# Seven block products instead of row products in the second attention layer of six images

## The chip, the cores and the metric

The kernel runs on one core of a Trainium2 chip. Its time is the device time of one execution in microseconds (us). Three runs of the kernel before gave 2307.95, 2308.07 and 2308.5 us; the median, 2308.07 us, is the time that the change is measured against. TensorE is written PE, VectorE DVE, ScalarE ACT, GpSimd POOL and SyncE SP, as in the profile.

## What is computed

Eight images of 32 x 32 positions (N = 1024 rows) and C = 256 channels pass two attention layers, all in fp32. Layer 0 has four heads of width 256; Layer 1 has one head with keys and queries of width 32 (Ck) and a gate gamma:

```
# layer 0: q, k, v = split(x W_qkv) per head
a   = softmax(q k^T * C**-0.5);  x1 = concat_h(a v) W_out + b_out + x
# layer 1
f, g, h = x1 Wf + bf, x1 Wg + bg, x1 Wh + bh
s   = softmax(g f^T);  out = gamma * (s h) + x1
```

## The kernel before

The work goes image by image. Layer 0 treats each head in two blocks of 512 queries (blk 0 and 1). Its three large products, scores, products with the rows of x, and output projection, are each done as seven block products instead of eight (Strassen-Winograd), by `seven` (L235). Its three tasks `one`, `two`, `three` multiply into three banks of PSUM named z, y and x (in the profile psz, psy, psx with the tile's name behind: psz_y for the products, psz_o for the output projection); ACT copies the first results out (L278, L279, L286), and DVE adds bank and copy into the output tile (L272). The sums of blocks that such a product needs as operands are made on DVE: `query_sums` (qs, L555), `sums` of the exponentials (tile ss, L614), sums of y (tile yt, L692), each 256 or 1024 values wide per partition.

The sum of exponentials over the keys of a block takes a long way in Layer 0: DVE adds over the key tiles (rs, L621, L625), POOL adds over the partitions (`partition_all_reduce` into rb, L627), a DMA on SP writes one row of that into DRAM (line, L631), a second one reads it back as four columns (st, L634), DVE inverts them (`invert`, L643), a DMA writes the inverses back to DRAM (inv, L648), and one more spreads that row over the 128 partitions (invb, L650). Then DVE multiplies the projected tile by it (L701), and POOL's DMA adds it onto x1 in transposed form (x1T, L704). SP issues in order; a DMA that waits for another holds all behind it. Of the buffers rs, rb, invb, ss and m0 there is one each, of s, v, q, y and st two.

Layer 1 of image b-1 is put between heads 1 and 2 of image b (behind all four heads in the last image, and at the very end for image 7). x1T is turned into rows of x1 (`turn_back`: SP's DMAs at L382 and transposes on DVE at L394). `queries_apart` (L751) multiplies x1 by Wf and Wg together; the result is spread by DMAs. `values` (L796) multiplies x1 by Wh, and DVE writes gamma times the result plus gamma times bh into v, with a column of ones beside it (L804). `scores` (L810) has two tasks per block. Each is four matmuls that use 32 rows of the array each, into four of the six PSUM banks "ps"; ACT takes the exponential of each bank into s (L830). `row_products` (L902) then takes, per group of 128 queries, eight matmuls of 257 columns (256 of v and the ones, L909), so that the sum of exponentials comes out in column 257; DVE inverts it (L917) and adds the scaled product to the rows of x1 (the line behind it); the store to the output follows from `done`.

The order on PE, DVE and ACT is written out by hand. A loop goes through the steps (unit, block); in each one `put(tasks, *positions)` places tasks at positions of a scale from 0 to about 10, and the tasks are issued sorted by position. Each step issues its own scores, the products of the step before (`one`), and the projection of the step before that (`two`). For image b the steps are h0 and h1 (both blocks each), Layer 1 of image b-1 (both blocks), h2, h3. SP and POOL get their DMAs in the order in which the tasks issue them.

At the end `judge` and `decide` count whether all inverses lie inside given bounds (FAR for Layer 1); if not, a general path is run.

Of the kernel before, what the change touches and what calls it, by code (L numbers as in the profile page):

```python
# [20 lines left out]
def kernel(  # L21
# [67 lines left out]
    FAR = 2.0**64  # L89
# [265 lines left out]
    xT_of, x1T_of, xblocks, vblocks = {}, {}, {}, {}  # L355
# [81 lines left out]
    def value_sums(b):  # L437

        made = {}

        def piece(i):
            if i == 0:
                r = rows[b]
                t = tile_of("xt", [P, 4, NT // 2, P], f"xt_{b}")
                blocks = [r[:, ts(j, NT // 2), ts(c, P)] for j in range(2) for c in range(CC)]
                sums = [t[:, k] for k in range(4)]
                made["l"] = sum_b(sums, *blocks)
                vblocks[b] = b_operands(blocks, sums)
            made["l"][i]()

        return [partial(piece, i) for i in range(4)]
# [58 lines left out]


    class Layer0:
# [82 lines left out]
        def sums(self, blk):  # L595


            n = f"{self.name}_{blk}"
            tt = nc.vector.tensor_tensor
            made = {}  # L600

            def start():
                half = NT // 2
                p = self.p[blk]
                blocks = [p[:, ts(j, half), ts(e, HB)] for e in range(2) for j in range(2)]
                t = tile_of("ss", [P, 2, half, HB], f"ss_{n}")
                sums = [t[:, 1], t[:, 0], blocks[2], t[:, 0]]
                self.pblocks[blk] = a_operands(blocks, sums)
                made["t"], made["l"] = t, sum_a(sums, *blocks)

            def piece(i):
                if i == 0:
                    start()
                made["l"][i]()  # L614

            def add(k):
                t = made["t"]
                if k == 1:
                    made["r"] = tile_of("rs", [P, 2, HB], f"rs_{n}")
                r = made["r"]  # L620
                tt(r, t[:, :, 0, :] if k == 1 else r, t[:, :, k, :], ALU.add)  # L621

            def last():
                r = made["r"]
                tt(r[:, 0, :], r[:, 0, :], r[:, 1, :], ALU.add)  # L625
                self.total[blk] = t = tile_of("rb", [P, NB], f"rb_{n}")
                nc.gpsimd.partition_all_reduce(  # L627
                    t, r.rearrange("p e i -> p (e i)"), P, bass_isa.ReduceOp.add
                )
                line = tile_of("line", [1, NB], f"line_{n}")  # L630
                nc.sync.dma_start(line, t[0:1, :])  # L631
                self.r[blk] = st = tile_of("st", [P, HT], f"st_{n}")
                with nc.allow_non_contiguous_dma(reason="a row of sums turns into columns"):
                    nc.sync.dma_start(st, line.rearrange("o (t p) -> p (o t)", p=P))  # L634

            adds = [partial(add, k) for k in range(1, NT // 2)]
            return [partial(piece, i) for i in range(4)], adds + [last]

        def invert(self, blk):

            n = self.first + blk * HT
            inv = inverse[:, n : n + HT]
            nc.vector.reciprocal(inv, self.r[blk])  # L643
            if blk in self.rb:
                return
            line = tile_of("line", [1, NB], f"inv_{self.name}_{blk}")
            with nc.allow_non_contiguous_dma(reason="columns turn into a row"):
                nc.sync.dma_start(line.rearrange("o (t p) -> p (o t)", p=P), inv)  # L648
            self.rb[blk] = t = tile_of("invb", [P, NB], f"invb_{self.name}_{blk}")
            nc.sync.dma_start(t, line[0].partition_broadcast(P))  # L650
# [6 lines left out]
        def products(self, blk):  # L657


            def out(c, e):  # L660
                if blk not in self.y:
                    self.y[blk] = tile_of("y", [P, CC, NB], f"y_{self.name}_{blk}")
                return self.y[blk][:, c, ts(e, HB)].unsqueeze(1)

            return seven(
                f"y_{self.name}_{blk}", HB, 1,
                lambda number: [
                    (0, vblocks[self.b][number][:, j, :], self.pblocks[blk][number][:, j, :])
                    for j in range(NT // 2)
                ],  # L670
                {
                    "11": partial(out, 0, 0), "12": partial(out, 1, 0),
                    "21": partial(out, 0, 1), "22": partial(out, 1, 1),
                },
                NARROW,
            )
# [42 lines left out]
    class Layer1:  # L719
        scale = 1.0  # L720

        def __init__(self, b, direct=0):

            self.b, self.name, self.direct = b, f"{b}_l1", direct
            self.s = {}
            self.fg, self.v = None, None

# [23 lines left out]
        def queries_apart(self, tag=None):  # L751
# [7 lines left out]
            def task():  # L759
                fg = self.fg_tile()  # L760
                self.f, self.g = fg[:, 0, :], fg[:, 1, :]
                if tag is None:
                    self.v = values_tile(f"v_{self.name}")
                    made["t"] = t = self.v.rearrange("p t c -> p (t c)")[:, :NB]
                else:
                    made["t"] = t = tile_of(tag, [P, NB], f"fg2_{b}")
# [29 lines left out]
        def values(self, last="psm"):  # L796
            def start():
                if self.v is None:
# [5 lines left out]
                lambda t2, pm: nc.vector.scalar_tensor_tensor(  # L804
                    self.v[:, 2 * t2 : 2 * t2 + 2, :C], pm, gamma_sb,
                    bh_sb.unsqueeze(1).broadcast_to([P, 2, C]), ALU.mult, ALU.add,
# [40 lines left out]
        def products(self, blk):  # L847
            return row_products(self, blk, rows1)

# [116 lines left out]
    steps, adds, exps = [], {}, {}  # L966

    for b in range(B):
        units = [Layer0(b, h) for h in range(HEADS)]
        if b > 0:  # L970
            units.insert(behind(b), Layer1(b - 1, NBLK))
        steps += [(u, blk) for u in units for blk in range(NBLK)]
# [9 lines left out]
    first_sums = value_sums(0)  # L982
# [10 lines left out]
    for i, (a, blk) in enumerate(steps):  # L993
# [7 lines left out]

        if l0:
            tasks, exps[i] = a.scores(blk)
            put(tasks, 0, 2, 4, 6, 8, 10)
            put(exps[i][:2], 5.1, 6.1)
        else:
            tasks, _ = a.scores(blk)
            put(tasks, *((0.5, 2.4) if blk == 0 else (0.5, 2)))
        if is_l0(two):
            u, k = two  # L1010
            put(u.products_of[k][2:], 1 if l0 else 0)
            if nxt is None:
                put([partial(u.invert_all, k)], 2.2)
            put([partial(u.invert, k)], 3.4 if l0 else 2.7)
            ysums, tasks, adds[i] = u.project(k)
            put(ysums, *((1.1, 1.2, 1.3, 3.3) if l0 else (1.1, 1.2, 1.3, 2.5) if blk == 0 else
                         (0.6, 0.7, 0.8, 0.9)))
            put(tasks, *((3, 5.5, 7) if l0 else (4.5, 6, 7.2) if blk == 0 else
                         (3, 5, 7) if nxt else (1.9, 3.1, 4.1)))
            if nxt is None:  # L1020
                put(adds[i], 4.2)
        if i - 1 in exps:
            put(exps[i - 1][2:], *((0.9, 0.91) if l0 else (0.1, 0.2)))
        if i - 1 in adds:
            put(adds[i - 1], 0.5 if l0 or blk == 1 else 2.3)
        if is_l0(one):
# [3 lines left out]
            put(sums, *((2.1, 3.2 if is_l0(two) else 2.4, 4.2, 5.6) if l0 else (0.8, 2.2, 3.5, 6.1)))  # L1030
            put(keys, *((6.3, 6.6, 7.6, 8.7) if l0 else (6.3, 7.6, 8.3, 8.7)))
            put(u.products_of[k][:2], *((5, 9) if l0 else (4, 5)))
        elif one is not None:
            put(one[0].products(one[1]), *((3, 5, 7, 9) if l0 else (1, 4, 6, 8) if nxt else (1, 3, 4, 8.5)))
# [3 lines left out]
        if i == 1:  # L1038
            put(first_sums[2:], 1.4, 3.4)
            put(fold[2], 0.5, 2.6, 3.5, 5.5, 7.5)  # L1040
            put([partial(nc.vector.tensor_scalar, bh_sb, bh_sb, gamma_sb, None, ALU.mult)], 8.5)

        if l0 and blk == 0:
            put(a.query_sums(1), 3.5, 4.3, 4.4, 5.3)
        if is_l0(nxt) and blk == NBLK - 1:
            put(nxt[0].queries(), *((2.5, 4.5, 6.5) if not l0 else
                                    (1.5, 2.5, 4.5) if is_l0(two) else (0.5, 2.5, 5.5)))
            put(nxt[0].query_sums(0), *((6.7, 6.9, 7.3, 7.6) if not l0 else
                                        (5.4, 6.4, 7.2, 7.4) if is_l0(two) else (6.4, 7.2, 7.3, 7.4)))
# [3 lines left out]
        if l0 and a.h == 0 and blk == 1 and a.b > 0:  # L1053
            put(value_sums(a.b), 1.4, 2.4, 3.4, 4.4)
        if l0 and a.h == 1 and blk == 0 and a.b + 1 < B:
            load_x(a.b + 1)
        if is_l0(nxt) and nxt[0].h == 2 and nxt[1] == 0 and nxt[0].b + 1 < B:
            moves, turned = turn_rows(nxt[0].b + 1)
            put(moves[:4], 1, 2.5, 4, 5.5)
        if l0 and a.h == 2 and a.b + 1 < B:  # L1060
            if blk == 0:
                put(moves[4:], 0.5, 1.5, 2.5, 3.5)
                put(turned, 6.4, 7.4, 8.4, 9.4)
            else:
                put(key_sums(a.b + 1), 0.5, 0.6, 6.4, 7.4)

        if l0 and a.b > 0 and a.h == behind(a.b) - 1:
            if blk == 0:
                moves, turned1 = turn_back(a.b - 1)
                put(moves[:4], 3, 4.5, 6, 7.5)  # L1070
            else:
# [3 lines left out]
                put(moves, 1.6, 1.7, 1.8, 1.9)  # L1075
        if not l0 and blk == 0:
            put(a.values("ps"), 0.9, 1, 2.3, 3, 6.5)
            put(turned1, 2.5, 2.9, 4.2, 5.1)
        for _, _, t in sorted(places, key=lambda x: x[:2]):
# [151 lines left out]
```

## Time and profile before

| | |
|---|---|
| median of the runs | 2308.07 us |
| profiled execution: time | 2307.59 us |
| profiled execution: span | 2305.4 us |
| granted TensorE clock | 1.00 |
| PE busy | 2296.3 us, 10256 records |
| DVE busy | 1507.7 us, 2663 |
| ACT busy | 758.9 us, 1297 |
| POOL busy | 319.9 us, 206 |
| all-reduces on POOL | 64 of 3.23 us |

The span is the time from the first to the last instruction; 2.2 us of the execution lie outside it. An fp32 matmul leaves two records, so 10256 records are 5128 matmuls. The matmuls overlap in part: the distance between two starts (the pitch), and not the length of a record, is what a matmul costs. In a timeline a row is a run of the same instruction: start, time from its start to its end, engine, line, operation, output and input with shapes, and the number of records; in brackets stands how long the engine was idle before it, and who ended that.

### The profile page before, as it was taken

The numbers are of one execution on the slowest core, as the hardware profiler recorded it, in microseconds if no ns is written. First come the engines' busy times: TensorE is split into PE (matmuls) and PEld (weight loads), VectorE is DVE, ScalarE is ACT, GpSimd is POOL, SyncE is SP. The second block draws the span as 40 slices with busy tenths as digits, with TensorE's granted clock in tenths as the row PEclk, the third lists the DMA queues.
The fourth block names the chain that finished last, engine by engine and source line by source line (L and its number), as shares of the span: only waits on it lengthen the run. The fifth ranks groups of instructions, "written<-read, shape, count | busy, mean of one in ns | idle before, by whom it ended". The sixth has DMA issues, their size and how long they took to land.

```text
span 2305.4 us, 27193 instructions
## 1 busy us (share of the span) xinstructions
PE 2296.3 (100%) x10256; PEld 1890.9 (82%) x10256; DVE 1507.7 (65%) x2663; ACT 758.9 (33%) x1297; POOL 319.9 (14%) x206
## 2 busy tenths in 40 slices
PE   9999999999999999999999999999999999999999
PEld 7888888788888888878887888878888788888887
DVE  6676776476765766656765566656676556776664
ACT  3333333233332333323333233322333233333322
POOL 0111112011120112101121011210112101111211
PEclk9999999999999999999999999999999999999999
DMA  4211112301223013220132211322013211121222
GB/s 137 33 28 28 27 33 49 75 15 28 42 46 67 15 28 52 42 61 15 28 57 40 59 15 28 58 38 59 19 28 54 46 33 19 28 46 26 38 41 65
DMA packets 240379, 94.81 MB, mean 41 GB/s; under 512 B 204464, under 2 KB 209456, under 8 KB 240240
## 3 DMA queue, kind: packets, MB, share of 16 engines
q1 hardware_dynamic: 220784, 55.23, 12.1%
q0 software_dynamic: 19456, 37.76, 9.3%
q8 instruction: 83, 1.36, 0.4%
q14 instruction: 56, 0.46, 0.1%
HBM read 29.76 MB, written 8.65 MB: 17 GB/s over the span
## 4 chain that ended last, share of the span: by engine, by line
PE 99%; ACT 1%; DVE 0%; issue 0%; ACTq 0%
PE psy_y L255 14%; PE psz_y L255 14%; PE psz L255 14%; PE psy L255 14%; PE pa_l L909 10%; PE psz_o L255 7%; PE psx_y L255 5%; PE psx L255 5%; PE psz_q L255 4%; PE psy_q L255 4%; PE pr_v_l L494 3%; PE ps_l L821 1%; PE psx_q L255 1%; PE psx_o L255 1%; PE pm_fg L771 1%; ACT x1T L459 0%
## 5 line engine op out<-in xcount | busy, mean ns | idle before, releaser
L627 POOL PARTITION_ALL_REDUCE rb<-rs x64 | 206.6, 3228 | 1463.0 <-issue 1078.9
L576 ACT ACTIVATE p<-p 128x1024 f32<-128x1024 f32 x256 | 263.9, 1056 | 71.4 <-DVE p L272 71.2
L255 PE MATMUL psz<-q,xs 128*128 128x256 f32 x1024 | 264.5, 381 | 0.0
L255 PE MATMUL psy<-qs,xs 128*128 128x256 f32 x1024 | 262.8, 379 | 0.0
L255 PE MATMUL psy_y<-p,xt 128*128 128x256 f32 x1024 | 241.9, 379 | 0.0
L909 PE MATMUL pa_l<-v_l,s_l 128*128 128x257 f32 x1024 | 232.1, 381 | 0.0
L255 PEld LDWEIGHTS psz<-q,xs 128*128 128x128 f32 x1024 | 192.8, 190 | 46.8 <-issue 19.1
L909 PEld LDWEIGHTS pa_l<-v_l,s_l 128*128 128x128 f32 x1024 | 193.7, 190 | 34.3 <-issue 6.8
L278 ACT COPY e<-psz 128x512 f32<-128x512 f32 x128 | 75.1, 587 | 437.3 <-PE psz L255 437.3
L255 PEld LDWEIGHTS psy_y<-p,xt 128*128 128x128 f32 x1024 | 194.6, 190 | 26.4
L255 PEld LDWEIGHTS psy<-qs,xs 128*128 128x128 f32 x1024 | 193.6, 190 | 27.4
L272 DVE TENSOR_TENSOR p<-psy,v 128x512 f32<-128x512 f32 x128 | 88.1, 688 | 85.1 <-ACT v L286 44.9
L704 POOL DMA_DIRECT2D x1T<-o x64 | 78.1, 1220 | 405.9 <-DVE o L701 345.2
L255 PE MATMUL psy<-qs,x0T 128*128 128x256 f32 x512 | 131.4, 379 | 0.0
L255 PE MATMUL psx<-q,x0T 128*128 128x256 f32 x512 | 131.4, 379 | 0.0
L255 PE MATMUL psz<-q,x0T 128*128 128x256 f32 x512 | 131.4, 379 | 0.0
L255 PE MATMUL psz_y<-ss,xt 128*128 128x256 f32 x512 | 121.0, 379 | 0.0
L255 PE MATMUL psx_y<-p,x 128*128 128x256 f32 x512 | 121.0, 379 | 0.0
L255 PE MATMUL psz_y<-ss,x 128*128 128x256 f32 x512 | 121.0, 379 | 0.0
L255 PE MATMUL psy_y<-ss,xt 128*128 128x256 f32 x512 | 121.0, 379 | 0.0
L255 PE MATMUL psz_y<-p,x 128*128 128x256 f32 x512 | 121.0, 379 | 0.0
L255 PEld LDWEIGHTS psz_y<-p,x 128*128 128x128 f32 x512 | 97.3, 190 | 20.9 <-issue 4.3
(146 smaller groups left out, 3689.5 us busy)
## 6 DMA issues: line engine op xcount, KB each, us to landing
x1T<-o POOLq DMA_DIRECT2D x64, 512.0 KB, 5.0
invb<-inv SPq DMA_DIRECT2D x63, 256.0 KB, 4.8
x<-x1T SPq DMA_DIRECT2D x256, 32.0 KB, 2.0
out_dram<-x SPq DMA_DIRECT2D x15, 512.0 KB
x<-in_x_dram SPq DMA_DIRECT2D x14, 512.0 KB, 4.4
x0T<-x SPq DMA_DIRECT2D x224, 32.0 KB, 2.3
fg<-v_l POOLq DMA_DIRECT2D x56, 64.0 KB, 2.0
w<-in_L_conv_W_qkv_dram SPq DMA_DIRECT2D x4, 512.0 KB, 7.5
```

The source lines that it names most:

```text
L255: nc.tensor.matmul(banks[k][:, ts(i, w)], lhsT=lhsT, rhs=rhs, start=first and n == 0, stop=True, skip_group_check=True,)
L272: nc.vector.tensor_tensor(dst, shaped(banks[k]), shaped(other), ALU.add)
L278: nc.scalar.copy(scratch("e"), banks["z"])
L494: nc.tensor.matmul(pm[:, ts(j, C)], lhsT=src()[:, c, ts(2 * t2 + j, P)], rhs=w()[:, c, :], start=(c == 0), stop=(c == CC - 1),)
L576: exp(both, both)
L627: nc.gpsimd.partition_all_reduce(t, r.rearrange("p e i -> p (e i)"), P, bass_isa.ReduceOp.add)
L704: nc.gpsimd.dma_start(x1T_of[self.b][:, :, ts(blk, NB)], o, accum_op=ALU.add)
L771: nc.tensor.matmul(pm[ts(k, half)], lhsT=w[:, c, :], rhs=x1T_of[b][:, c, ts(k, NB)], start=(c == 0), stop=(c == CC - 1),)
L821: nc.tensor.matmul(pm, lhsT=self.f[ts(r, CK), ts(j0 + r, P)], rhs=self.g[ts(r, CK), ts(blk, NB)], start=True, stop=True,)
L909: nc.tensor.matmul(pm[:, : C + 1], lhsT=p[:, j, ts(ti, P)], rhs=v[:, j, : C + 1], start=(j == 0), stop=(j == NT - 1),)
```

## The change

Layer 1 of images 0 to 5 no longer makes values first. Since s (x1 Wh) = (s x1) Wh, it multiplies s by the rows of x1, as seven block products, and projects the result by Wh (already scaled by gamma) behind that. Image 6's and image 7's Layer 1 keep the old way.

```diff
+        if 0 < b < B - 1:
+            u = Layer1(b - 1, NBLK, True)
+            order[NBLK * behind(b) : NBLK * behind(b)] = [(u, 0)]
+            order[NBLK * behind(b) + 2 : NBLK * behind(b) + 2] = [(u, 1)]
```

So the steps are now h0, h1, (Layer 1, blk 0), (h2, blk 0), (Layer 1, blk 1), (h2, blk 1), h3. Block products combine two halves of the queries, whose sums of exponentials differ by many powers of two; so the second half of the queries is first scaled to the sums of the first half. The sums can't come from a column of ones any more, and `weigh` makes them as Layer 0 does:

```diff
+        def weigh(self, blk):
+            def add(k):
+                s = self.s[blk]
+                if k == 1:
+                    made["r"] = tile_of("rs", [P, NB], f"rs_{n}")
+                tt(made["r"], s[:, 0, :] if k == 1 else made["r"], s[:, k, :], ALU.add)
+            def total():
+                made["c"] = sums_to_columns(made["r"], n)
+            def invert():
+                k = (self.b * NBLK + blk) * HT
+                st, half = made["c"], HT // 2
+                self.inverse[blk] = inv = inverse1[:, k : k + HT]
+                nc.vector.reciprocal(inv, st)
+                tt(st[:, half:], st[:, :half], inv[:, half:], ALU.mult)
+                made["i"] = row_of(st[:, half:], n)
+            def scale(k):
+                q = NT // 2
+                s = self.s[blk][:, ts(k, q), HB:]
+                tt(s, s, made["i"].unsqueeze(1).broadcast_to([P, q, HB]), ALU.mult)
```

`sums_to_columns` holds the all-reduce and the two DMAs (line, st), `row_of` the two DMAs inv and invb, both taken out of Layer 0's code; for Layer 1 inv holds 256 values and invb is 256 wide. `block_sums` and `block_products` are Layer 0's four sums of 1024 and its call of `seven`, taken out likewise; the other operand are the rows of x1 with four block sums of 512 (tile x1s, made by `value_sums`). The projection:

```diff
+        def project(self, blk):
+            def start():
+                made["o"] = o = tile_of("m0", [P, HT, C], f"out_{self.name}_{blk}")
+                nc.vector.tensor_tensor(
+                    o, rows1[self.b][:, ts(blk, HT), :],
+                    bh_sb.unsqueeze(1).broadcast_to([P, HT, C]), ALU.add,
+                )
+            def task(t2):
+                pm = tile_of("psm", [P, NB], f"po_{self.name}_{blk}_{t2}")
+...
+                        nc.tensor.matmul(
+                            pm[:, ts(j, C)],
+                            lhsT=y[:, c, ts(2 * t2 + j, P)],
+                            rhs=wh_sb[:, c, :],
...
+                for j in range(2):
+                    o = made["o"][:, 2 * t2 + j, :]
+                    nc.vector.scalar_tensor_tensor(
+                        o, pm[:, ts(j, C)], self.inverse[blk][:, j : j + 1], o, ALU.mult, ALU.add
+                    )
```

Many positions move. Those of the step loop that matter most here, in this order: Layer 1's scores (in the lines of `else`), the row sums, the inverse of Layer 0, its product of o and invb (`adds`), and the new parts (`new` is a step of the changed Layer 1):

```diff
-            put(tasks, *((0.5, 2.4) if blk == 0 else (0.5, 2)))
+            put(tasks, *((0.5, 0.65) if blk == 0 or new else (0.5, 2)))
+        if new:
+            tasks, scales[i] = a.weigh(blk)
+            put(tasks, 6.596, 6.696, 6.952, 7.396, 7.496, 7.596, 7.696, 7.796)
-            put([partial(u.invert, k)], 3.4 if l0 else 2.7)
+            put([partial(u.invert, k)], 7.05 if not l0 else 3.4 if one is None or is_l0(one) or not one[0].blocks else 4.049)
-            put(adds[i - 1], 0.5 if l0 or blk == 1 else 2.3)
+            put(adds[i - 1], -0.178 if l0 or blk == 1 or new else 2.342)
+        elif one is not None and one[0].blocks:
+            u, k = one
+            u.products_of[k] = u.block_products(k)
+            put(scales[i - 1], 1.709, 4.05, 4.1)
+            put(u.sums(k), 4.564, 4.664, 5.764, 6.514)
+            put(u.products_of[k][:2], 6, 9)
+        elif two is not None and two[0].blocks:
+            u, k = two
+            put(u.products_of[k][2:], 0.157 if l0 else 0)
+            start, tasks = u.project(k)
+            put(start, 2.3)
+            put(tasks, *((3, 5.5) if l0 else (4.767, 6)))
```

FAR goes from 2^64 to 2^60, and wh_sb is scaled by gamma as bh_sb was.

## The prediction

> **What bounds the kernel now.** I read four views, in this order: the page's busy shares, the chain that ended last, the timeline of TensorE (PE) around one Layer 1 step, and the timelines of VectorE (DVE) and of SyncE's DMA queue (SP) around one inverse.
>
> ```profile
> PE 2296.3 (100%) x10256; PEld 1890.9 (82%) x10256; DVE 1507.7 (65%) x2663; ACT 758.9 (33%) x1297; POOL 319.9 (14%) x206
> PE 99%; ACT 1%; DVE 0%; issue 0%; ACTq 0%
> ```
>
> PE never rests, so time is the sum of matmul pitches (start to start) as long as nobody is late for it. But DVE's 65% is a mean: in the 25 us from 376 to 401, around a Layer 1 step, the windows view gives DVE 18.24 us, from 470 to 500 it gives 23.41 of 30. A change that packs more DVE work before a matmul that needs it meets a limit the mean doesn't show.
>
> ```profile
> 375.38 1.14 PE L821 MATMUL ps_l<-fg 32*128 32x512 f32 x8
> 376.45 3.72 PE L494 MATMUL pr_v_l<-wh_sb,x1T 128*128 128x256 f32 x16
> 380.10 1.14 PE L821 MATMUL ps_l<-fg 32*128 32x512 f32 x8
> ...
> 440.06 3.63 PE L909 MATMUL pa_l<-v_l,s_l 128*128 128x257 f32 x16
> 443.52 1.03 PE L255 MATMUL psz<-q,xs 128*128 128x256 f32 x4
> ...
> 500.13 1.89 PE L255 MATMUL psy_y<-p,xt 128*128 128x256 f32 x8
> 501.86 1.89 PE L255 MATMUL psx_y<-p,x 128*128 128x256 f32 x8
> ```
>
> Each fp32 matmul is two records, so x8 is four matmuls: 501.86 - 500.13 = 1.73, or 0.431 us for one of 256 columns; 443.52 - 440.06 = 3.46 for eight of 257 columns, 0.433 each. A score task of four row-packed matmuls takes 1.07 (375.38 to 376.45).
>
> ```profile
> 489.62 0.37 SPq L648 DMA_DIRECT2D inv<-inverse  x1
> 498.11 0.34 SPq L650 DMA_DIRECT2D invb<-inv  x1
> ...
> SPq L650 <- DMA inv<-inverse: 498.9, 63, 12.1
> ```
>
> This is the row that will matter most. The inverse of a sum is turned into a row by one transfer (inv) and spread over the partitions by a second (invb), which waits on SP until the first has landed: 8.5 us here, in all 63 cases 498.9 us, 7.9 each. From inv's issue to invb's the trace has 7.8 at least, 8.4 in the median; invb then lands 3.1 at least, 4.8 in the median after its issue. With 0.2 from the reciprocal to the issue, reciprocal to usable row is 11.1 to 13.4 us. Before, DVE uses that row (L701) 16 to 26 us after the reciprocal (489.42 to 506.12 in this step), so nobody sees it.
>
> **The change part by part.**
>
> *Matmuls taken out.* Per image 64 matmuls of 257 columns become 56 of 256; the 16 value projections are replaced by 16 output projections of the same size. 64 x 0.433 - 56 x 0.431 = 3.5 us, on PE's path; six images: 21 us. If nothing else moved: 2307.6 (the profiled run; 0.5 under the median of 2308.07) - 21 = 2286.
>
> *Score tasks side by side.* The second task moves from behind sixteen value matmul records to right behind the first. The eight result tiles have six banks: in the built order matmuls 7 and 8 wait for the first two exponentials. These start 1.16 after the first score matmul (376.54 on ScalarE) and last 0.6, pitch 0.48, so the eighth matmul starts at 2.3, and the next full one at 2.3 + 1.07 = 3.4, 3.6 with the mode change. Before, the two tasks cost 2 x 1.27 (1.07 and about 0.1 on each side). That is +1.03 us for a pair; two pairs in each of six images and one in Layer1(6): 13 x 1.03 = 13.4 us. The 0.1 at each end is in the trace, before the first score matmul and behind the last. The page TensorEngine Tiling (Array Packing) of the Trainium skill, section Key Properties, says that a change of tiling mode drains TensorE; by that rule alone, priced with the 0.2 of the trace, the adjacent pairs would save 13 x 0.2 = 2.6 us. The figure of 1.03 already has that saving in it.
>
> *DVE work added ahead of the new products.* Per block: seven adds of 512 (row sums), a reciprocal and a product, two scalings of 1024, four block sums of 1024, a bias add of 1024, four scalar-tensor-tensors of 256; four sums of x1's blocks per image. Removed are the value evacuations and eight reciprocal and eight row updates per image. I count time from the first score matmul of (l1, blk 0) in images 1 to 6. PE reaches psy_y of the new products, which needs their second block sum, at 36.4. Before it DVE has, from that zero (the instruction before it needs the last matmul before the scores), 66 instructions: 10 of 1024 at 1.135 (380.40 to 381.54 to 382.67), 26 of 512 at 0.60 or, if one needs the one before, 0.72, 26 of 256 at 0.33 or 0.46, four tiny ones at 0.1:
>
> ```profile
> 397.23 0.42 DVE L272 TENSOR_TENSOR o<-psz_o,u_o 128x256 f32<-128x256 f32 x1
> 397.56 0.42 DVE L272 TENSOR_TENSOR o<-psz_o,e_o 128x256 f32<-128x256 f32 x1
> 397.89 1.41 DVE L621 TENSOR_TENSOR rs<-rs,ss 128x512 f32<-128x512 f32 x2
> ...
> 400.38 2.86 DVE L701 TENSOR_TENSOR o<-o,invb 128x1024 f32<-128x1024 f32 x1
> ```
>
> 11.4 + 17.2 + 9.6 + 0.4 = 38.6 us against 36.4: DVE alone is over 2 us late with no wait at all.
>
> *The two inverse chains in that stretch.* This is the dear part. DVE runs in order. The reciprocal for (h1, blk 0), moved from position 2.7 to 7.05, is its 26th instruction: about 18.0, since q's last parts come from PE at 15.2 and three row sums follow (0.6 + 0.6 + 2 x 0.72). Its consumer, o times invb, is only fourteen instructions and some 6.5 us of work behind it, but the row needs 11.1 to 13.4: it starts at 29.1 to 31.4, and DVE stands still for 5 to 7 us. Queued behind it are the sums of (h1, blk 1) that PE's psz_o needs, and then all of Layer 1. On SP the new line and st transfers stand behind that invb, so st lands at about 30, in time. Resuming at 30.2 (the middle): 3.2 for o and the y sums, 0.2 for reciprocal and product, 0.2 to the issue of the new inv at 33.8. That transfer has 256 values, not 512; no row shows it. Bounds: st, the other small transfer, 2.1, and inv itself, 7.8 to 8.4; I take 5.0, the middle, and 3.9 for invb, between 3.1 and 4.8. The scaling starts at 42.7, having hidden 5.9 us of other DVE work; from there 6.0 us (two scalings, two sums of 1024, four of 256) to the sum PE waits for: 48.7, 12.4 us late. With all lower bounds 44.4 (8.0 late), with the upper ones 54.2 (17.8).
>
> *Block 1* (zero at its first score matmul). The row sums wait for the buffer that the all-reduce of (h2, blk 0) reads, until about 14.3; seven adds 5.0, all-reduce 3.2, line and st 3.3: reciprocal at 26.0; 0.2 and 8.9 as above: scaling at 35.1; 7.7 us of DVE to the last block sum: 42.8, where PE wants it at 37.6: 5.2 late (1.7 to 9.5 by the bounds).
>
> *A DVE operation beside an all-reduce.* The 2.86 us row above (1.215 usually) ran while POOL's all-reduce stood from 399.93 to 403.16; 7 of 64 such operations are stretched. Twelve all-reduces are new, and the one of (l1, blk 0) falls on four q sums of 256; I price it at 0 to 1 us a block, inside the bounds above. The page SBUF — State Buffer, section Who interferes with whom, has a VectorE instruction with two SBUF inputs and a GpSimd read exclude each other, the later one fully blocked. Fully blocked until 403.16, the 1.215 us would have ended at 404.4; it ended at 403.24. By the page the q sums would end some 2 us later still. Either way they stand between the reciprocal and o times invb, where DVE waits for the row anyway.
>
> *At nothing:* POOL's and ACT's extra work (14% and 33% busy); output DMAs, which end behind the store before; the moved sums of Layer 0 steps. Those use o times invb about 2 us earlier, 14 to 17 us behind the reciprocal, against 11.1 to 13.4: the cover holds by 1 to 5 us, and if it is gone costs DVE that time in steps where it has slack. FAR narrows to 2^60; the sums of exponentials of these inputs lie between 2^15 and 2^49, so the general path isn't taken.
>
> **Sum.** Per image 12.4 + 5.2 + 2.06 - 3.54 = 16.1; six: 96.7; the last pair 1.0; together 97.7 on 2307.6: **2405**. All lower bounds: 8.0 + 1.7 + 2.06 - 3.54 = 8.2, 2358. All upper: 25.8, 2464.
>
> **Rivals.**
>
> *PE's count rules* (the other side). If DVE gets through its 66 instructions in 36.4 us (0.55 each, not 0.58) and both rows are there when asked for, 21 us come off less the 13.4 of the bank waits: 2300; without those 2286. It decides where reciprocal to row is under 6.5 us. For it: PE is 100% busy and its own sum falls. Against it: the shortest of 63 chains is 11.1.
>
> *DVE's load only.* If the rows come early enough, per image there is 2.2 (load) + 0.9 (block 1's buffer) + 2.06 - 3.54 = 1.6 to 2.5: 2318 to 2324. Against it: the same 63 chains.
>
> *Stalls beyond this.* PE resting some 12 us might restart at a lower clock; the first 16 records of the program have 214 ns against 109 later. At 1.7 us for each long stall, +10 to 20: 2415 to 2425. The clock row is 9s throughout, so this is open.
>
> *The change does not do what it says:* in the built order there are 48 fewer matmuls and twelve more all-reduces. Excluded, but for 1 in 100.
>
> **How the numbers follow.** A measurement can tell 0.2% from no change, 4.6 us: same is 2303.5 to 2312.7. Waits for the rows (with or without the slow restart): 0.70, 2358 to 2464, most below 2445. Load and short waits: 0.16, 2313 to 2358. PE's count: 0.11, 2286 to 2303. What lies between: 0.03. The range 2320 to 2445 leaves out the faster cases and thin ends on both sides. Faster 0.11, same 0.03, slower 0.86.
>
> **What would show it.** PE's share falls under 97%, with idle time before psy_y and psz_o released by DVE in images 1 to 6 and none in the last image's Layer 0 steps. DVE shows 5 to 7 us idle before o times invb in (l1, blk 0) and some 3 before the scaling, ended by the invb transfer. In steps without Layer 1 PE keeps its pitch. I am wrong if reciprocal to row is much under 11 us in these steps, if the 256-value inv takes as long as one of 512 (then the upper end), or if PE shows no idle time of microseconds.

## The result, and the profile after

The changed kernel takes **2557.63 us** (median of six runs, 2556.13 to 2561.38) against 2308.01 for the kernel before on the same chip: ratio 1.108, 95% interval 1.107 to 1.110. The forecast was 2405 with a range to 2445. The direction and the place were right; the loss is two and a half times the size.

The changed kernel's page, first busy time, then the slices of PE and of its granted clock, then the chain:

```profile
PE 2338.4 (91%) x10160; PEld 1912.4 (75%) x10160; DVE 1661.4 (65%) x2856; ACT 774.7 (30%) x1333; POOL 358.0 (14%) x212
PE   9999996899968999689996899978899888999989
PEclk9999998999989999899998999999899998999999
PE 71%; DMA 16%; DVE 8%; issue 3%; POOL 2%; SPq 1%; ACT 0%; DVEq 0%; POOLq 0%
```

PE has 96 records fewer (48 matmuls) and still 42 us more of busy time: the four slices with a 6 for PE, one in each of the first four Layer 1 stretches, have an 8 for the clock beside them, and so have two of the slices with an 8. The mean clock is 0.959, where it was 1.00. The chain, which was 99% PE, now runs through DMAs for 16% of the span. DVE's share is the 65% that it was: a mean over the span tells nothing of this loss.

Who PE waited for, over the whole span (us in total, times, longest):

```profile
PE psy_y_l L255 <- DVE ss_l L549: 144.7, 12, 14.5
PE psz_o L255 <- DVE yt L709: 26.9, 7, 8.8
PE psy L255 <- DVE qs L617: 16.6, 6, 3.0
PE psy_y L255 <- DVE ss L549: 13.8, 6, 3.5
PE psy_y L255 <- DVE y L272: 7.0, 6, 1.2
```

What DVE itself waited for in Layer 1, in the same form:

```profile
DVE s_l L899 <- DMA invb_l<-inv_l: 113.0, 12, 13.2
```

And the first block of Layer 1 of image 0 (its first score matmul is at 375.09; these are the rows behind a wait), PE above, DVE's waits in the middle, SP's part of the chains below, from 357 on:

```profile
385.21 2.42 PE L255 MATMUL psy_y<-ss,xts 128*128 128x256 f32 x8 [3.06 <-DVE ss L549]
...
416.73 0.70 PE L255 MATMUL psz_o<-yt,wo 128*128 128x256 f32 x2 [4.30 <-DVE yt L709]
417.27 1.87 PE L255 MATMUL psz<-q,xs 128*128 128x256 f32 x4
...
437.67 3.70 PE L255 MATMUL psy_y_l<-ss_l,x1s 128*128 128x256 f32 x8 [12.08 <-DVE ss_l L549]
441.21 0.59 PE L255 MATMUL psz_o<-y,wo 128*128 128x256 f32 x2
```

```profile
379.98 1.23 DVE L718 TENSOR_TENSOR o<-o,invb 128x1024 f32<-128x1024 f32 x1 [4.36 <-DMA invb<-inv]
...
413.41 1.23 DVE L718 TENSOR_TENSOR o<-o,invb 128x1024 f32<-128x1024 f32 x1 [7.58 <-DMA invb<-inv]
...
431.56 2.36 DVE L899 TENSOR_TENSOR s_l<-s_l,invb_l 128x1024 f32<-128x1024 f32 x2 [8.66 <-DMA invb_l<-inv_l]
```

```profile
357.04 6.35 SPq L809 DMA_DIRECT2D fg<-x1s  x8
363.43 1.29 SPq L386 DMA_DIRECT2D x0T<-x  x2
364.82 0.54 SPq L530 DMA_DIRECT2D inv<-inverse  x1
...
399.60 0.46 SPq L530 DMA_DIRECT2D inv<-inverse  x1
409.80 0.34 SPq L532 DMA_DIRECT2D invb<-inv  x1
...
416.99 0.36 SPq L530 DMA_DIRECT2D inv_l<-st_l  x1
426.35 0.33 SPq L532 DMA_DIRECT2D invb_l<-inv_l  x1
```

The chain can be read from the bottom up. PE stands 12 us before psy_y_l because DVE's sum ss_l is late; that is late because DVE stood 8.7 us for invb_l; and invb_l was issued 9.4 us behind inv_l, a transfer of 256 single values. Behind the wait four matmuls take 437.67 to 441.21, 0.88 us each and not 0.43: PE comes back at half speed, and the granted clock of these 3.5 us is 0.50, against 1.00 from 441.21 to 455. The same stands at 417.27 (x4 is two matmuls in 1.66 us).

**Where 251 us come from.** The spans differ by 2556.4 - 2305.4 = 251.0 us. From the distances between the starts of all matmuls behind the first 60 us, against the usual distance of their shape (waits are distances over it by more than 0.7 us; the sum of the forecast is the prediction's, from unrounded parts):

| part | forecast | measured |
|---|---|---|
| 48 matmuls fewer | -21.2 | -21.2 |
| score tasks side by side | +13.4 | +15.6 (52.9 us of score tasks, 37.3 before) |
| waits in block 0, six images | +74 | +128 |
| waits in block 1, six images | +31 | +78 |
| waits in the last image | 0 | +10 |
| matmuls at a lower clock behind waits, and small ones | 0 | +41 |
| sum | 98 | 251 |

### The profile page after: what moved, and what is told of

Same layout as the page of the kernel before. It is cut to its first block, busy times and chain, and to the rows that moved or that the text cites. A ratio compares the mean times of both kernels' runs of the same rounds, so it can differ in the third digit from the quotient of the medians.

```text
span 2556.4 us, 27385 instructions
## 1 busy us (share of the span) xinstructions
PE 2338.4 (91%) x10160; PEld 1912.4 (75%) x10160; DVE 1661.4 (65%) x2856; ACT 774.7 (30%) x1333; POOL 358.0 (14%) x212
## 4 chain that ended last, share of the span: by engine, by line
PE 71%; DMA 16%; DVE 8%; issue 3%; POOL 2%; SPq 1%; ACT 0%; DVEq 0%; POOLq 0%
PE psz L255 11%; PE psy L255 11%; PE psy_y L255 10%; PE psz_y L255 10%; DMA inv<-inverse 6%; PE psz_o L255 5%; DMA inv_l<-st_l 4%; PE psx L255 4%; PE psy_y_l L255 3%; PE psx_y L255 3%; DMA invb<-inv 2%; DMA invb_l<-inv_l 2%; PE psz_q L255 2%; PE psy_q L255 2%; PE pa_l L1004 2%
## 5 line engine op out<-in xcount | busy, mean ns | idle before, releaser
L638 ACT ACTIVATE p<-p 128x1024 f32<-128x1024 f32 x256 | 257.2, 1052 | 61.3 <-DVE p L272 61.1
L255 PE MATMUL psy_y<-p,xts 128*128 128x256 f32 x1024 | 243.0, 380 | 7.0 <-DVE y L272 7.0
L255 PEld LDWEIGHTS psy_y<-p,xts 128*128 128x128 f32 x1024 | 194.5, 190 | 35.8 <-DVE y L272 9.4
L255 PE MATMUL psy_y_l<-ss_l,x1s 128*128 128x256 f32 x96 | 44.2, 641 | 144.7 <-DVE ss_l L549 144.7
L255 PEld LDWEIGHTS psy_y_l<-ss_l,x1s 128*128 128x128 f32 x96 | 30.2, 330 | 155.7 <-issue 149.2
L549 DVE TENSOR_TENSOR ss<-p,ss 128x1024 f32<-128x1024 f32 x64 | 78.2, 1222 | 101.3 <-PE psy_y L255 101.3
L255 PE MATMUL psy_y<-ss,xts 128*128 128x256 f32 x512 | 125.7, 390 | 13.8 <-DVE ss L549 13.8
L718 DVE TENSOR_TENSOR o<-o,invb 128x1024 f32<-128x1024 f32 x64 | 77.9, 1218 | 74.0 <-DMA invb<-inv 73.9
L255 PEld LDWEIGHTS psy_y<-ss,xts 128*128 128x128 f32 x512 | 99.0, 194 | 29.7 <-issue 16.0
```

Source lines behind the costliest of these rows:

```text
L255: nc.tensor.matmul(banks[k][:, ts(i, w)], lhsT=lhsT, rhs=rhs, start=first and n == 0, stop=True, skip_group_check=True,)
L638: exp(both, both)
L718: nc.vector.tensor_tensor(o, o, self.rb[blk].unsqueeze(1).broadcast_to([P, CC, NB]), ALU.mult)
```

## The experiments

Theory 1 is the prediction's: PE waits for DVE, and DVE for the two chains of transfers behind an inverse. Rivals: DVE has too much work whatever the transfers do; the score pairs; and, new with the result, the lower clock as a cost of its own. The first five experiments are one run each; ten runs of one of the later kernels lie up to 5.7 us apart, so differences of that size say nothing here.

**The ratio made on DVE.** The all-reduce leaves the sums on all partitions, so the row of ratios needs no transfer (`t` is now rb; the inverse of the columns, which the projection uses, is made behind the scaling):

```diff
...
-                nc.vector.reciprocal(inv, st)
-                tt(st[:, half:], st[:, :half], inv[:, half:], ALU.mult)
-                made["i"] = row_of(st[:, half:], n)
+                made["i"] = i = tile_of("invb", [P, HB], f"invb_{n}")
+                nc.vector.reciprocal(i, t[:, HB:])
+                tt(i, i, t[:, :HB], ALU.mult)
...
```

> The changed kernel, but the ratio that the scaling multiplies by is made on DVE from rb itself, which holds the sums on every partition (a reciprocal of 256 and a product of 256, some 2 us by the 3.34 us that the last block's reciprocal of 512 takes); inv_l and invb_l are gone, and the inverse of the columns comes behind the scaling. Theory 1, the two transfers behind Layer 1's inverse make PE wait (12.2 to 13.6 and 9.2 to 14.7 us before psy_y_l): the scaling starts some 7 us earlier in block 0, where the row of (h1, blk 0) still has to be waited for, and some 8 us earlier in block 1, so about 15 to 18 us an image less, 2450 to 2470 us, and psy_y_l waits under 6 us in block 0 and under 2 in block 1. Theory 2, DVE simply has too much work: 2 us of DVE time more per block make it 2557 to 2580 us.

Measured: 2420.41 us, 137 less, and 30 under the range of theory 1. PE's waits for Layer 1's sums:

```profile
PE psy_y_l L255 <- DVE ss_l L549: 38.7, 12, 5.5
```

144.7 became 38.7 us with 2 us of DVE work more in each block. The two transfers, with the waits and the low clock that followed from them, are the largest part of the loss; that DVE's load alone is the reason has fallen. What is left in block 0 (5.5 us in most images) is not gone with these transfers: there DVE still stands 5.5 to 7.8 us for Layer 0's row.

**Layer 0's inverse back at 2.7.**

```diff
-            put([partial(u.invert, k)], 7.05 if not l0 else ...
+            put([partial(u.invert, k)], 2.7 if not l0 else ...
```

> The changed kernel with Layer 0's inverse in steps of Layer 1 back at position 2.7 (7.05 in the changed one). Theory 1, the row of (h1, blk 0) comes 7.6 us too late for o times invb in block 0 and 11.0 us too late in the last image: these two waits go, PE's wait at psz_o (1.5 to 4.5 us) goes, psy_y_l of block 0 is reached sooner, and the last image loses its 9.0 us wait: 2490 to 2515 us. Theory 2, the row's lateness is set by SP's queue (x0T transfers ahead of it) and not by the position of the reciprocal: o times invb is still ended by the invb transfer, 2545 to 2558 us.

Measured: 2525.69 us, 32 less, between the two. DVE's waits for Layer 0's rows, the changed kernel first, then this one:

```profile
DVE o L718 <- DMA invb<-inv: 73.9, 14, 11.0
```

```profile
DVE o L718 <- DMA invb<-inv: 29.9, 11, 3.8
...
DVE inverse L683 <- DMA st<-line: 12.9, 6, 3.3
```

The last image's wait of 9.0 us is gone, as expected. In Layer 1's steps part of the wait only moved: the earlier reciprocal now has to wait for its own sums (st), and its inv stands on SP behind thirteen x0T transfers of 0.65 us each (385.34 to 393.78 in this run's trace). So both theories hold a part: the position, and the queue.

**The score tasks apart in the changed kernel** (second task at 2.4, not 0.65).

> The changed kernel with the second score task of Layer 1 at 2.4, not beside the first. Theory 1, the pair's 1.03 us each are a cost of their own on PE's path (prediction): 12 to 13 us less, 2544 to 2547 us. Theory 2, PE waits for DVE behind the scores in the same step anyway, and what PE gains it then waits: 2553 to 2560 us, with the score tasks themselves shorter (1.27 each) and the waits at psy_y_l longer by as much.

Measured: 2532.86 us, 25 less, outside both ranges, but the score tasks themselves fell by 3.4 us only (49.5 against 52.9): at this place the second task takes 1.41 us, and PE waits 0.4 us more behind it for an exponential. Most of the rest is shorter waits, and the inv transfers were shorter too (9.2 us from inv to invb in the mean, 9.9 in the changed kernel), which this edit doesn't touch. Inconclusive: between two kernels that both wait for these rows, a difference of this size can come from the transfers alone.

**The wait filled with matmuls.**

```diff
+                for _ in range(fill if k == "y" else 0):
+                    product(k, 1, True)
                 product(k, number, k != "y" or not two_banks)
```

> The changed kernel with extra matmuls in the wait before psy_y_l: the four matmuls of the first block product are repeated six times in block 0 and five times in block 1 into the bank that psy_y_l starts anew, 10.4 and 8.6 us, so that PE doesn't stand still. Theory 1, behind a wait of over some 3 us PE runs at half speed for about 3.4 us (the eight matmuls behind psy_y_l take 0.43 us more each, 1.5 to 1.7 us in all): with the wait filled they run at full pitch and the kernel becomes 12 to 20 us shorter with 132 us of matmuls more, 2537 to 2546 us. Theory 2, the slow matmuls have another cause (their own operands, fresh from DVE): they stay slow, 2556 to 2570 us.

Measured: 2506.82 us, 51 **less with 264 matmuls more**, 30 under the range of theory 1. PE around psy_y_l of the same block (the x48 are the filler and the first block product):

```profile
421.78 10.52 PE L255 MATMUL psy_y_l<-s_l,x 128*128 128x256 f32 x48
433.26 1.99 PE L255 MATMUL psy_y_l<-ss_l,x1s 128*128 128x256 f32 x8 [0.96 <-DVE ss_l L551]
435.10 0.59 PE L255 MATMUL psz_o<-y,wo 128*128 128x256 f32 x2
```

The four matmuls behind the filler take 433.26 to 435.10, 0.46 each, where they took 0.88: the doubled distances came from standing still, not from their operands. Over the kernel slow and small distances fall by 22 us. The remaining 29 us are waits: filler and waits together make 187 us, the waits before 216, and inv to invb is 9.2 us in the mean here. How much of those 29 is a producer that runs earlier because PE isn't slowed, and how much the transfers, stays open.

**Both edits of the first two.**

> The ratio row made on DVE and Layer 0's inverse back at 2.7, the edits of the two earlier runs together. Theory 1, the waits are two chains one behind the other in block 0, so that with both gone DVE is late there by its load alone (2 to 5 us): 2355 to 2385 us, o times invb waits for no more than 2 us in Layer 1's steps, and PE's waits come to some 60 us in all. Theory 2, the two edits save the same wait twice: 2400 to 2420 us.

Measured: 2415.04 us, 5 under the first alone, no more than runs of one kernel differ by: theory 2. DVE's waits for Layer 0's rows fell from 56.2 to 31.9 us, but PE's waits stayed (92.6 us, 92.0 in the first experiment): psy_y_l still stands 5.5 us in most images. Up to the sum that psy_y_l needs, DVE is busy for 42 us, stands 2.9 to 4.1 us for Layer 0's row and up to 3.2 us for its st. How the 5.5 us divide between DVE's work, its order and these waits, this run doesn't show.

**Another order of the tasks**, same matmuls, ratio made on DVE in place. The core of the edit:

```diff
-            put([partial(u.invert, k)], 7.05 if not l0 else 3.4 if ... else 4.049)
+            put([partial(u.invert, k)], 2.7 if not l0 and not new else 2.49 if not l0 else -0.287 if ... else 1.114)
-            put(adds[i - 1], -0.178 if l0 or blk == 1 or new else 2.342)
+            put(adds[i - 1], 1.546 if l0 and is_l0(one) else -0.17 if l0 and one is not None and one[1] == 0 else 0.204 if l0 else -1.268 if new and blk == 0 else ...)
-            put(tasks, 6.596, 6.696, 6.952, 7.396, 7.496, 7.596, 7.696, 7.796)
+            put(tasks, *((6.596, 7.77, 8.026, 8.47, 8.57, 8.67, 8.77, 8.87) if blk == 0 else ...))
-            put(value_sums(rows1, ...), 2.288, 2.388, 2.488, 3.288)
+            put(value_sums(rows1, ...), -0.97, -0.04, 2.488, 4.704)
```

> The ratio row made on DVE, in place in rb, and the tasks of the steps put in another order, chosen so that no engine comes late: Layer 0's inverses earlier and their products with o later or earlier as their rows allow, the row sums of block 0 and of x1 spread out, the fg moves ahead. The matmuls are those of the changed kernel. Theory 1, everything that the change lost, it lost to waits behind DVE's order and the transfers, and to the slow matmuls behind them: without waits the 21 us of matmuls are there, less up to 13 of the score pairs, 2290 to 2312 us, clock 0.99 to 1.00. Theory 2, DVE has too much work around Layer 1 for any order: 2330 to 2370 us with waits at psy and psy_y_l in each image.

Measured: 2328.64 us, ratio 1.009 (1.007 to 1.011), clock 1.00. Of the 251 us, 230 were order and transfers, with the low clock that follows waits. No wait before psy_y_l is over 0.5 us any more; neither theory's range holds the time, which lies between them. Left are 21 us of short waits and 14 us of score pairs (51.6 against 37.3). A likely cause of one of the short waits shows on DVE and POOL:

```profile
688.33 2.04 DVE L617 TENSOR_TENSOR qs<-q,qs 128x256 f32<-128x256 f32 x1
```

```profile
687.84 3.23 POOL L516 PARTITION_ALL_REDUCE rb_l<-rs_l  x1 [7.32 <-DVE o L272]
```

The q sum takes 2.04 us instead of 0.42 beside the new all-reduce. DVE has no gap from there to the sum p for which PE waits 1.2 us at 697.52; no run took this stop alone away.

**Further positions moved.**

> The kernel of the run before with further positions moved (the x1s sums, the fg moves and the y sums of Layer 0 among them), so that the two to three short waits of PE that are left in each image (21 us in all) shrink. Theory 1, what is left over the kernel before is these waits and the score pairs (14 us), against 21 us of matmuls saved: with the waits cut to 10 to 15 us, 2308 to 2322 us. Theory 2, the remaining waits come from all-reduces that hold DVE up and move with them wherever they are put: 2324 to 2335 us.

Measured: 2324.36 us, ratio 1.007 (1.006 to 1.009): at the edge of theory 2. The waits are 19.7 us in place of 21.3; this edit settled little.

**Row sums of block 1 behind the y sums, score tasks apart.** Core of the edit:

```diff
-            put(tasks, *((0.5, 2.4) if not new and blk == 0 else (0.65, 0.93) if blk == 0 else (0.5, 0.651) if new else (0.5, 2)))
+            put(tasks, *((0.5, 2.4) if not new and blk == 0 else (0.65, 1.06) if blk == 0 else (0.5, 4.1) if new else (0.5, 2)))
-            put(tasks, *(... else (6.596, 6.696, 6.952, 7.396, 7.496, 7.596, 7.697, 7.797)))
+            put(tasks, *(... else (10.346, 10.446, 10.702, 11.146, 11.246, 11.346, 11.447, 11.547)))
```

> The kernel of the run before with three edits: the row sums of block 1 stand behind the y sums (before, their first add held DVE until an all-reduce had ended, and PE waited 1.3 us for the y sum behind it, in each of six images), Layer 1's two score tasks stand apart with q's (block 0) or y's (block 1) first products between them, and a few positions follow. Theory 1, the waits and the pairs are costs of their own on PE's path: 7.5 us less for the waits and 12 us less for the pairs, 2300 to 2308 us, about the kernel before or under it. Theory 2, DVE is the bound there, and what is taken from one wait comes back in the next: 2316 to 2325 us.

Measured: 2312.86 us, ratio 1.0023 (1.0013 to 1.0032): the nearest that was reached to the kernel before, and still over it. The 1.3 us wait for the y sum is gone from all six images, as theory 1 says; the total is some 5 us over its range. PE around the score tasks, and who PE still waits for:

```profile
660.50 1.14 PE L843 MATMUL ps_l<-fg 32*128 32x512 f32 x8
661.57 1.12 PE L255 MATMUL psz_q<-x0T,wqk 128*128 128x512 f32 x2
662.53 1.02 PE L255 MATMUL psy_q<-xs,wt 128*128 128x512 f32 x2
663.49 1.41 PE L843 MATMUL ps_l<-fg 32*128 32x512 f32 x8
665.29 1.99 PE L255 MATMUL psz_y<-p,x 128*128 128x256 f32 x8 [0.40 <-ACT s_l L852]
```

```profile
PE psy L255 <- DVE p L272: 7.8, 6, 1.4
PE psz_o L255 <- DVE yt L709: 4.0, 6, 1.1
```

The balance over the kernel before: 21.2 us of matmuls saved, against 12.9 of waits, 4.7 of score tasks and 8.0 of small distances. The 11.8 us in the second fence, 2 us an image, come in block 0, where DVE runs from 677 to 702 with one gap of 1 us: there DVE's work sets the time. The sum p that frees the bank for PE's longest wait (1.4 us) stands directly behind the ratio's reciprocal and product (690.68 to 692.88), the 2.2 us that the first experiment's edit put on DVE; whether another place for p would end the wait was not tried.

**The same with the score tasks side by side**, nothing else moved.

> The same kernel with Layer 1's score tasks side by side in the twelve blocks, and nothing else moved. Theory 1 (the prediction's term of 1.03 us a pair): 12 to 13 us more than with the tasks apart, all of it in the score matmuls (3.5 us a pair in place of 2 x 1.27). Theory 2, the pair saves two mode changes and the exponentials come earlier, which DVE needs: 0 to 5 us more, or less than with the tasks apart.

```profile
662.05 3.42 PE L843 MATMUL ps_l<-fg 32*128 32x512 f32 x16
665.39 1.13 PE L255 MATMUL psz_q<-x0T,wqk 128*128 128x512 f32 x2
```

Measured: 2319.27 us, 6.4 more, and the runs of the two kernels don't overlap (2316.59 to 2320.70 against 2310.62 to 2316.30). It lies between the two ranges. The pair takes 662.05 to 665.39, 3.34 us, and the score tasks 9.2 us more in all (51.2 against 42.0), 0.8 a pair; 2.5 us come back, about what PE waited behind the second task (0.40 in the fence above, six times). The term is real; in time it is half of the forecast here because the tasks apart aren't free of bank waits either (1.41 and 0.40).

## Why the prediction was wrong

*Matmuls taken out, score pairs.* Right: the counts and pitches held, the pair costs 3.34 us and 0.1 at either end where 3.6 was forecast, 15.6 us in all for 13.4.

*The two chains.* The mechanism was right, instruction for instruction: the reciprocal of (h1, blk 0), the stand of DVE at o times invb, the second stand at the scaling. Every link that was read from a row held: 3.2 us from o times invb to the y sums (413.41 to 416.6), 6.0 from the scaling to the sum that PE needs (431.56 to 437.53), block 1's reciprocal at 26.7 for 26.0. What failed are three prices:

- "That transfer has 256 values, not 512; no row shows it ... I take 5.0". It takes 9.36 us in the mean of twelve (8.0 to 11.5), nearly as long as one of 512 (9.9). In the four runs that have both, half the values took 0.3 to 1.3 us less, not half the time. Its invb, "3.9", is 5.8 in the mean from issue to use (3.1 to 9.1, one of 10.8). 15.2 for 8.9, twelve times, is 75 us, by this sum the larger part of the 100 us that the waits in the two blocks exceed the forecast by. This is the term that failed most. The prediction named this as what would make it wrong, but gave it the upper end of the range, when the nearest row, the same transfer with twice the values, should have been the value.
- "At nothing: ... the moved sums of Layer 0 steps ... the cover holds by 1 to 5 us." It doesn't hold at the seam to Layer 1. The reciprocal of (h0, blk 1) at 355.32 gets its inv onto SP at 364.82: SP first issues eleven fg and x0T transfers, 0.6 to 0.8 us each. Over the six images this row waits 8.4 to 10.2 us for its issue; in the kernel before it waited 2.5 to 4.8 us at this place. "0.2 from the reciprocal to the issue" is the free queue's time. So DVE stands 4.4 us at the start of block 0, and the reciprocal that was to stand at 18.0 stands at 23.0. PE's first wait in the block (1.5 to 3.7 us) is this one. The same line put the last image at nothing, whose inverse moved to 7.05 too: 9.0 us, gone when it moved back.
- *Stalls beyond this.* The slow restart was a rival with a price, 1.7 us a long stall, and left out of the sum. It comes: 1.2 to 3.1 us behind each stall over 3.5 us, 41 us in all with small ones, for the 10 to 20 of the rival: there are three to five stalls over 1.9 us an image, not two, and some cost more than 1.7.

*DVE's load.* The amount was about right: from the first score matmul to the end of the second block sum DVE is busy 39.7 to 40.0 us in the six images, for 38.6, with a stop of 1.1 beside an all-reduce in it. That this alone makes PE "over 2 us late" no run shows, since with the built order DVE always waited for rows too; in the other orders no wait before psy_y_l is over 0.5 us. The 2 us an image of the last but one experiment come at other matmuls, with 2.2 us of the ratio's work on DVE, so that the same figure comes out is chance.

*A DVE operation beside an all-reduce* was read as a stretch. It is a stop, see below. It holds the q sums of block 0 up by 1.1 us (402.30 in the block shown), where 0 to 1 was forecast.

*PE's count rules* (2300) didn't come; the best order, at 2312.86 us, is 13 us short of it.

## What to carry to other kernels

A chain of small transfers is priced by the rows of the same kind of transfer, the longest included, not by its bytes, and from the moment at which the queue is free to issue it. When two such chains stand behind each other on an in-order engine, the later one starts from the first one's end: add them up, then ask which value already lies where it is needed (here the sums, on all partitions). Count the stalls that come out and price each with the slow restart.

## What the runs showed of the hardware

*The clock after a wait.* Over all ten kernels (the changed one and nine experiments), with waits counted as in the table above: of 147 waits of PE between 0.7 and 1.9 us none started slow matmuls; of 72 between 1.9 and 3.5 us 36 did; of 59 above 3.5 us all did. Slow means twice the pitch, and where it was looked up a granted clock of 0.50 (417.27 to 420.64 and 437.67 to 441.21). Behind nearly all of the long waits the slow stretch begins at once and lasts 3.0 to 6.1 us; behind most of the shorter ones it begins 0.5 to 1.5 us later and lasts 3.0 to 3.5. The Trainium skill's page TensorE: Matmul & The Clock Gate, section What's actually happening, tells of a free-running window of about 3.4 us and half speed after an idle one. The shorter stretches agree with that length, the longest are nearly two windows; and waits from 2.1 us on, shorter than one window, are followed by half speed too.

*All-reduce and DVE.* A DVE operation with both inputs in SBUF that starts in the first 2 us of an all-reduce ends, less its own usual time, 2.1 us behind the all-reduce's start in each of four cases: 400.38 + 2.86 - 1.215 against 399.93 before the change, 402.30 + 1.49 - 0.42 against 401.27 in the changed kernel, 688.33 + 2.04 - 0.42 against 687.84 above, 687.55 + 1.07 - 0.42 against 686.10 in the last order. Of 80 such operations in all eleven traces 69 give 2.09 to 2.11 us, the others up to 2.7; none of 1071 with an input in PSUM took longer than usual there. The numbers fit an operation that stands still for the first 2.1 of the 3.23 us and then runs at full speed, as far as the profile's times on POOL, which are rough, can tell. That is nearer to the full block of the page SBUF — State Buffer, section Who interferes with whom, than to the prediction's reading, but the block ends 1.1 us before the all-reduce.
